# Keys scaled ahead of the scores, feed-forward sums tied to later tiles, attended sums by pairs, and a split exponential in a decoder layer

## The chip, the cores and the metric

The kernel runs on one core of a Trainium2 chip. The metric is the device time of one launch in microseconds (us); lower is better. The times of the kernel before are 1092.79, 1094.14 and 1094.13 us, median 1094.13. The profile is of one more execution.

The core has a matrix engine (TensorE, rows PE for matmuls and PEld for the loads of their stationary operand), VectorE (DVE), ScalarE (ACT), GpSimd (POOL) and SyncE (SP), which here only issues DMAs. Each engine works through its own queue in order; semaphores order the engines against each other. Matmuls write to PSUM banks, which TensorE, VectorE and ScalarE reach.

## The reference, cut to what matters

One decoder layer, post-norm, for 2 batches of 512 tokens of width 512, all in float32:

```python
# self attention: 16 heads of 128, weights = codes * block scales
q, k, v = x @ wq + bq, x @ wk + bk, x @ wv + bv
attn = softmax(q @ k.T / sqrt(128))            # per head, 512 x 512
x = layernorm(x + (attn @ v) @ wo + bo)
# cross attention over 1024 memory rows, one head of 512
scores = coef * (x @ Wq.T) @ mem.T
scores = scores - max(scores)
thr = top_k(scores, 54)[..., -1:]              # the 54th largest of each row
att = softmax(where(scores < thr, -inf, scores))
x = layernorm(x + (att @ mem) @ Wo.T)
# feed-forward, 2048 wide
gate, up = split(x @ w_gate_up.T)
x = layernorm(x + (silu(gate) * up) @ w_down.T)
```

## The kernel before, in words

**Products with seven blocks.** Almost every matrix product goes through `seven` (L170 to 229). It cuts both operands in 2 x 2 blocks and makes the product of the blocks with seven block products instead of eight. Four extra sums of blocks are needed for the left operand (`combine_a`, L107 to 110) and four for the right one (`combine_b`, L116 to 119); they run on GpSimd or VectorE ahead of the product. The seven products go into four half banks: product 1 starts the bank `r`, products 6 and 7 add to it; products 2, 5 and 4 go into three parts of a double bank `z`, and product 3 adds to one of them. After each of the products 1, 6 and 7 ScalarE copies `r` to SBUF with a bias (`keep` 0, 1 and 2, L197; the tiles are named u, for instance uqk). Product 3 of one call is left open (`open_product`) and is done by `close` inside the next call, after its product 6, so that it need not wait. VectorE then adds z and u: `on_second` makes one half of the result, `on_first` the other. In the profile the rows of L187 are these products: rqk, zqk for queries and keys, rv and zv for values, ro and zo for the output product, rxq and zxq for the query of the cross attention, rgu and zgu for the feed-forward's gate and up, rpd and zpd for its down product.

**Self attention.** 32 units: 4 groups of 4 heads by 2 batches are 8 phases of 4 units. For each unit:
- `queries_keys` (L736): one call of `seven` makes the key k (add at L747, from keep 2) and the query q (add at L748). The first unit has its own function with plain matmuls.
- `weights` (L770): four score matmuls sc (L784), two tiles of 128 x 512 to a double bank; VectorE takes the negated row maximum of both (L795), ScalarE multiplies it by `HSCALE` (L796, the 1/sqrt(128) of the reference), and makes the exponential with the same scale and that bias (L799, with a sum per row), VectorE the reciprocal (L807), ScalarE the normalised weights (L808). VectorE turns blocks of 32 x 32 (L811) and 16 DMAs finish the transpose (tq to pt, L819).
- `attend` (L825): the attended values av (L831) of an earlier unit; ScalarE copies them to ot (L849). `project` (L860) does the sums otc of four units' ot (L116 to 119) and the output product of a phase, added to the residual (L876, L878).

The double bank z of the products and the double banks of scores come from the same two buffers. A product that takes a buffer waits until the exponentials of the score tiles in it are done.

**Cross attention.** `seven_xquery` makes the query of a batch, from x1T (the turned residual) and x1c (its four sums, on VectorE); `qc` are the sums of the query (L142, L143), the right operand of the scores. `clip` (L483) finds the 54th largest score of each row by seven rounds of MAX8 (L487, L496) and six of MATCH_REPLACE8 (L493) on a 128 x 1024 tile; ScalarE makes the exponential (L500), VectorE keeps those over the threshold and sums them (L502), and ScalarE scales by the reciprocal (L506). Batch 0's search runs beside the self attention of batch 1, that of batch 1 (`search1`) beside the feed-forward of batch 0. `xattend` does the rest of it.

**Feed-forward.** For each batch two halves of 8 units. `up` (L1077) loads weights wgu (L1104), makes the sums wc on GpSimd (L107 to 110), calls `seven`, adds the up half ut (L1121) and the gate half gt (L1127), takes the Silu (L1129), multiplies (L1130) and makes the sums hc for the next product. `load_wdn` brings the down weights, `combine_wdn` (L1056) makes their sums dc on GpSimd (L1067 to 1074, eight of 128 x 512), and `down` (L1146) the product. The calls stand at L1198 to 1230; `next(between)` in `up` gives the sums of `combine_wdn` out a piece at a time.

**What sets the order.** The program is written with the functions above, but each engine's order is not the order of the text: a planner takes all instructions with their dependences and orders them by estimated times. An added dependence or a longer instruction in one place can therefore move others. Buffers are named by tags (`place`, `bank`, `double`), and a tag's next tile waits for the last reader of the one before.

ScalarE has its functions in tables: where Exp, Silu or Sqrt follow one another, an ACT_TABLE_LOAD stands between (rows of L500 and L1129 among them). Identity and Copy need none.

Of the kernel before, what the change touches and what calls it, by code (L numbers as in the profile page):

```python
# [24 lines left out]
def decoder_layer(  # L25
# [52 lines left out]
    def place(tag, shape, name):  # L78
        return sb.tile([P, *shape], F32, tag=tag, name=name)
# [87 lines left out]
        if open_product:  # L167
            open_product.pop()()

    def seven(name, stat, mov, cols, on_second, on_first, bias=(0.0, 0.0), late=False, piece=None):  # L170


        n = seven_count[0] % 2
        seven_count[0] += 1
        r = bank("r", f"r{name}")[:, :HS]
        if piece:

            zs = [bank("t", f"z{name}_{i}")[:, :HS] for i in range(2)] + [double(f"z{name}", (4, HS))[:, 2, :]]
        else:
            z = double(f"z{name}", (4, HS))  # L180
            zs = [z[:, i, :] for i in range(3)]
        u = place(f"u{n}", (3, HS), f"u{name}")

        def product(i, o, start=True):
            left, right = chunks(stat[i]), chunks(mov[i])
            for k in range(len(left)):
                nc.tensor.matmul(  # L187
                    o,
                    left[k][:, cols],
                    right[k],  # L190
                    start=start and k == 0,
                    stop=k == len(left) - 1,
                    skip_group_check=not start,
                )

        def keep(i, at):
            nc.scalar.activation(u[:, i, :], r, AF.Identity, bias=at)  # L197

        if late:
            product(2, zs[1])  # L200
            product(4, zs[0])
        product(1, r)
        keep(0, bias[0])
        if not late:
            product(2, zs[1])
        product(5, zs[2])
        product(6, r, False)
        keep(1, bias[0])
        close()
        product(7, r, False)  # L210
        keep(2, bias[1])
        if piece:
            piece(zs[2], u[:, 2, :], 1, 1)
            piece(zs[1], u[:, 0, :], 0, 0)
        if not late:
            product(4, zs[0])
        if piece:
            piece(zs[0], u[:, 2, :], 1, 0)
        else:
            on_second(z[:, 0::2, :], u[:, 2:3, :].to_broadcast([P, 2, HS]))  # L220

        def rest():
            product(3, zs[2], False)
            if piece:
                piece(zs[2], u[:, 1, :], 0, 1)
            else:
                on_first(z[:, 1:3, :], u[:, 0:2, :])

        open_product.append(rest)
# [252 lines left out]

    def clip(b, t, tag):  # L483

        s = sts[b, t]
        top = small.tile([P, 8], F32, tag="top", name=f"top{b}_{t}")
        nc.vector.max(top, s)  # L487
        mx = small.tile([P, 1], F32, tag="mx", name=f"mx{b}_{t}")
        nc.vector.tensor_scalar_mul(mx, top[:, 0:1], -1.0)
        work = place(tag, (M,), f"work{b}_{t}")  # L490
        src = s
        for r in range((CLIP_K - 1) // 8):
            nc.vector.match_replace(work, top, src, LOWEST)  # L493
            src = work
            top = small.tile([P, 8], F32, tag="top", name=f"top{b}_{t}_{r}")
            nc.vector.max(top, work)  # L496
            yield
        at = (CLIP_K - 1) % 8
        e = work
        nc.scalar.activation(e, s, AF.Exp, bias=mx)  # L500
        sm = small.tile([P, 1], F32, tag="xsm", name=f"xsm{b}_{t}")
        nc.vector.scalar_tensor_tensor(  # L502
            s, s, top[:, at : at + 1], e, ALU.is_ge, ALU.mult, accum_out=sm
        )
        nc.vector.reciprocal(sm, sm)
        nc.scalar.activation(s, s, AF.Copy, scale=sm)  # L506
        yield

    def clips(b, tags):
# [226 lines left out]
    def queries_keys(u):  # L736

        g, b, j = units[u]
        h = g * GH + j
        qt = place(f"q{u % 2}", (2, HS), f"q{u}")  # L740
        kt = place(f"k{u % 2}", (2, HS), f"k{u}")
        seven(
            f"qk{u}",
            qkw[u],
            xcs[b],
            slice(0, P),
            lambda z, c: nc.vector.tensor_add(kt, z, c),  # L747
            lambda z, c: nc.vector.tensor_add(qt, z, c),  # L748
            (bq_sb[:, h : h + 1], bk_sb[:, h : h + 1]),
        )  # L750
        qs[u], ks[u] = qt.rearrange("p n s -> p (n s)"), kt.rearrange("p n s -> p (n s)")

    def first_queries_keys():

        z = double("zqk0", (2, S))
        for k in range(KD):
            for n in range(2):
                nc.tensor.matmul(
                    z[:, n, :],
                    raw["qk0"][0][:, k, n, :],  # L760
                    xts[0][:, k, :],
                    start=k == 0,
                    stop=k == KD - 1,
                )
        qs[0] = place("q0", (S,), "q0")
        ks[0] = place("k0", (S,), "k0")
        nc.scalar.activation(qs[0], z[:, 0, :], AF.Identity, bias=bq_sb[:, 0:1])
        nc.scalar.activation(ks[0], z[:, 1, :], AF.Identity, bias=bk_sb[:, 0:1])

    def weights(u):  # L770

# [2 lines left out]
        for t in range(NT):  # L774
            if t % 2 == 0:

                if u == 0 and t:
                    pair = [bank("t", f"sc{u}_{t}_{n}") for n in range(2)]
                else:
                    scs = double(f"sc{u}_{t}")  # L780
                    pair = [scs[:, n, :] for n in range(2)]
                nms = small.tile([P, 2], F32, tag="nm", name=f"nm{u}_{t}")
                for n in range(2):
                    nc.tensor.matmul(  # L784
                        pair[n],
                        q[:, (t + n) * P : (t + n + 1) * P],
                        k,
                        start=True,
                        stop=True,
                    )  # L790
                if u == 0 and t:
                    for n in range(2):
                        nc.vector.reduce_max(nms[:, n : n + 1], pair[n], axis=AX.X, negate=True)
                else:
                    nc.vector.reduce_max(nms, scs, axis=AX.X, negate=True)  # L795
                nc.scalar.mul(nms, nms, HSCALE)  # L796
            pr = place(f"p{t}", (S,), f"p{u}_{t}")
            sm = small.tile([P, 1], F32, tag="sm", name=f"sm{u}_{t}")
            nc.scalar.activation(  # L799
# [1 line left out]
                pair[t % 2],  # L801
                AF.Exp,
                bias=nms[:, t % 2 : t % 2 + 1],
                scale=HSCALE,
                accum_out=sm,
            )
            nc.vector.reciprocal(sm, sm)  # L807
# [17 lines left out]
    def attend(u):  # L825
# [14 lines left out]
        if j % 2 == 0:  # L840
# [11 lines left out]
            AF.Identity,  # L852
            bias=bv_sb[:, h : h + 1],
        )

    def combine_o(eng, p):
        w = raw[f"o{p}"][0]
        ow[p] = combine_a(eng, blocks_t(w), place("wv" if p == last else "cmb1", (4, GH // 2, HD), f"oc{p}"))

    def project(p):  # L860

        g, b = phases[p]
        lo, hi = ots.pop((p, 0)), ots.pop((p, 1))
        oc = combine_b(
            nc.vector,
            (lo[:, :, :HS], lo[:, :, HS:], hi[:, :, :HS], hi[:, :, HS:]),
            place("cmb0", (4, GH // 2, HS), f"otc{p}"),
        )
        rr = rb[b].rearrange("p (h s) (c f) -> p h s c f", h=2, c=2)
        for s in range(NT // 2):  # L870

# [24 lines left out]
    for k in range(KD):  # L896
        nc.scalar.dma_start(out=first[0][k], in_=wqk_first[0][:, k])
        nc.sync.dma_start(out=xts[0][:, k, :], in_=xT[0, k * P : (k + 1) * P, :])
    nc.sync.dma_start(out=bqkv_sb, in_=bqkv)
    for n in range(2):  # L900
        nc.scalar.dma_start(out=first[1][n], in_=wqk_first[1][:, n * HK : (n + 1) * HK])
    for h in range(2):
# [140 lines left out]

    NH = NI // 2
    NQ = NH // 2
    wdns = {}

    def load_wdn(b, half):
        wdns[b, half] = []
# [3 lines left out]
            nc.sync.dma_start(out=t, in_=rows.rearrange("(i p) f -> p i f", p=P))  # L1053
            wdns[b, half].append(t)

    def combine_wdn(b, half):  # L1056

        b00, b01, b10, b11 = (f[:, :, h] for f in wdns[b, half] for h in (slice(0, HD), slice(HD, D)))
        c = []
# [3 lines left out]
            c += [two[:, 0], two[:, 1]]  # L1063
        wdns[b, half] = BRIGHT((b00, b01, b10, b11), c)
        steps = [slice(k, k + 2) for k in range(0, NQ, 2)]
        for w in steps:
            nc.gpsimd.tensor_tensor(c[0][:, w], b01[:, w], b00[:, w], ALU.subtract)  # L1067
            yield
# [8 lines left out]
    def up(b, half, eng, search=iter(()), between=iter(()), other=None):  # L1077
# [23 lines left out]
        for n in range(NH):  # L1101
# [10 lines left out]
            if other and n == NH - 1:  # L1112
                for _ in search:
                    pass
                for _ in other:
                    if sums:
                        sums.pop()()
            ut = place(f"k{n % 2}", (2, HS), f"ut{i}_{b}")

            def second(z, u, ut=ut):  # L1120
                nc.vector.tensor_add(ut, z, u)  # L1121
# [80 lines left out]
    seven_xquery(1, "xT1", "xc1", ("sc1", "p0"))  # L1202
    score_tiles(1, (("v0", 2), ("v1", 2)))
    seven_xscores(1)
    for _ in chain(combine_wdn(0, 0), combine_mem(1, ("wqk2", "sc2", "p2", "p3"))):
        pass
    search1 = clips(1, ("work",))
    hc = up(0, 0, nc.gpsimd, search1)
# [3 lines left out]
    def attended_early():  # L1212
        xw["woc"] = combine_b(nc.gpsimd, blocks(xw["wo"]), place("v1", (4, HK, HD), "woc"))
        yield from xattend(1, ("ot0", "ot1"))

    hc = up(0, 1, nc.vector, search1, combine_wdn(0, 1), attended_early())
    layernorm(1, "b")
    turn_x(1, "v0", "v1", "x2T")
    combine_turned(nc.vector, 1, "v0", "x2")
# [1 line left out]
    close()  # L1221
    finish(0)
    load_wdn(1, 0)
    hc = up(1, 0, nc.vector, between=combine_wdn(1, 0))
    down(1, 0, hc)
    load_wdn(1, 1)
    hc = up(1, 1, nc.vector, between=combine_wdn(1, 1))
    down(1, 1, hc, True)
    close()
    finish(1)  # L1230
# [68 lines left out]
```

## Time and profile before

| | |
|---|---|
| runs, us | 1092.79, 1094.13, 1094.14 |
| the profiled execution, us | 1093.0 |
| its span, us | 1090.8 |
| granted TensorE clock | 1.0 |
| VectorE, row maxima L795 | 63 of 1223 ns |
| ScalarE, scaling of maxima L796 | 64 of 202 ns |
| ScalarE, exponentials of the attention L799 | 128 of 685 ns |
| GpSimd, weight sums of the feed-forward L107 | 32 of 774 ns |
| VectorE, searches of the cross attention L496, L493 | 48 of 1221 ns, 40 of 1208 ns |
| ScalarE, exponential of the search L500 | 8 of 1152 ns |

The span is the time from the first to the last instruction that the profiler saw; the execution's time contains a little around it. A row of the views gives start and duration, engine, line, operation, the tile written and the tiles read, with partitions x elements. What stands in brackets is the idle time of the engine before it and what ended that. Some 36 of the 4290 matmul records are missing from this trace, so sums over matmuls are a little low.

By time the span has these parts: up to 540 us self attention with batch 0's cross attention in between; 540 to 735 the last units of the self attention and batch 1's cross query; 735 to 910 the feed-forward of batch 0 with batch 1's search; then the end of its cross attention and the feed-forward of batch 1.

### The profile page before, as it was taken

What the parts mean: (1) busy time and instruction counts of PE and PEld (TensorE: products, weight loads), DVE (VectorE), ACT (ScalarE), POOL (GpSimd) and SP (SyncE); (2) the same over time, 40 slices, a digit from 0 to 9 for tenths busy, and PEclk for the clock granted to TensorE, in tenths of its full rate; (3) what the DMA queues carried; (4) which work ended last, traced back from release to release, by engine and by line L of the source; (5) the groups of instructions that cost most, each with busy time, mean ns of one, the idle gap of its engine ahead of it and who ended that gap; (6) DMA issues with size and microseconds to landing.
All of it is one profiled execution on the core that took longest, in us unless ns stands there. A gap on an engine that the chain in (4) does not pass through costs nothing.

```text
span 1090.8 us, 12892 instructions
## 1 busy us (share of the span) xinstructions
PE 1074.4 (98%) x4254; PEld 798.2 (73%) x4254; DVE 636.6 (58%) x1043; ACT 416.6 (38%) x945; POOL 546.2 (50%) x546
## 2 busy tenths in 40 slices
PE   9999999999999999999999999989999999999997
PEld 6676776677677677665666567668888888888886
DVE  5445445346345445643899874568999736543354
ACT  3454435335344443733444453321443214221221
POOL 4965715845843844513852553651675812454620
PEclk9999999999999999999999999999999999999999
DMA  9634536554554355535332535431214401422201
GB/s 350 193 101 154 193 103 210 183 160 154 179 172 127 124 185 155 185 90 179 135 116 78 154 102 208 133 97 42 80 65 145 134 22 50 164 78 77 96 20 39
DMA packets 66256, 142.70 MB, mean 131 GB/s; under 512 B 12560, under 2 KB 12560, under 8 KB 66192
## 3 DMA queue, kind: packets, MB, share of 16 engines
q1 hardware_dynamic: 65328, 139.80, 40.2%
q10 hardware_dynamic: 864, 2.10, 0.5%
q8 instruction: 34, 0.56, 0.2%
q14 instruction: 30, 0.25, 0.1%
HBM read 99.90 MB, written 2.10 MB: 94 GB/s over the span
## 4 chain that ended last, share of the span: by engine, by line
PE 77%; DVE 14%; ACT 4%; DMA 2%; issue 1%; POOL 1%; ACTq 0%; DVEq 0%; POOLq 0%; SPq 0%
PE sc L784 9%; PE av L831 9%; PE zqk L187 8%; PE zgu L187 7%; PE rqk L187 6%; PE rgu L187 5%; PE zo L187 5%; PE zv L187 5%; PE ro L187 4%; DVE work L493 4%; DVE top L496 3%; PE zpd L187 3%; PE rv L187 3%; PE rpd L187 3%; PE zxav L187 2%; PE rxav L187 2%
## 5 line engine op out<-in xcount | busy, mean ns | idle before, releaser
L831 PE MATMUL av<-pt,v 128*128 128x512 f32 x256 | 121.8, 592 | 0.0
L784 PE MATMUL sc<-k,q 128*128 128x512 f32 x256 | 116.9, 597 | 0.0
L795 DVE TENSOR_REDUCE nm<-sc 128x2 f32<-128x1024 f32 x63 | 76.8, 1223 | 66.9 <-PE sc L784 66.9
L811 DVE STREAM_TRANSPOSE tq<-p 128x512 f32<-128x512 f32 x128 | 85.0, 698 | 35.1 <-ACT p L808 27.9
L107 POOL TENSOR_TENSOR wc<-wqk 128x256 f32<-128x256 f32 x31 | 24.2, 782 | 161.9 <-PE zqk L187 160.9
L784 PEld LDWEIGHTS sc<-k,q 128*128 128x128 f32 x256 | 47.6, 190 | 58.0 <-issue 50.9
L684 POOL TENSOR_TENSOR wqk<-wqk,sqk 128x512 f32<-128x512 f32 x52 | 65.1, 1273 | 47.7 <-DMA wqk<-in_wqk 28.2
L799 ACT ACTIVATE p<-sc,nm 128x512 f32<-128x512 f32 x128 | 86.9, 685 | 1.5
L808 ACT ACTIVATE p<-p,sm 128x512 f32<-128x512 f32 x128 | 86.1, 722 | 0.6 <-DVE sm L807 0.6
L107 POOL TENSOR_TENSOR wc<-wgu 128x256 f32<-128x256 f32 x32 | 24.8, 774 | 102.4 <-PE zgu L187 41.5
L197 ACT ACTIVATE ugu<-rgu 128x256 f32<-128x256 f32 x96 | 36.2, 379 | 103.7 <-PE rgu L187 101.5
L831 PEld LDWEIGHTS av<-pt,v 128*128 128x128 f32 x256 | 48.6, 190 | 30.5 <-issue 26.8
L197 ACT ACTIVATE uqk<-rqk,bqkv_sb 128x256 f32<-128x256 f32 x93 | 44.0, 473 | 64.9 <-PE rqk L187 64.8
L187 PE MATMUL rgu<-x2c,wc 128*128 128x256 f32 x256 | 66.1, 380 | 1.0 <-ACT ugu L197 1.0
L187 PE MATMUL rqk<-x0c,wc 128*128 128x256 f32 x248 | 64.8, 384 | 0.3
L187 PEld LDWEIGHTS rqk<-x0c,wc 128*128 128x128 f32 x248 | 45.5, 190 | 19.4 <-ACT uqk L197 10.0
L496 DVE MAX8 top<-work 128x8 f32<-128x1024 f32 x48 | 58.6, 1221 | 0.9
L187 PEld LDWEIGHTS rgu<-x2c,wc 128*128 128x128 f32 x256 | 48.3, 190 | 8.7 <-ACT ugu L197 1.6
L849 ACT ACTIVATE ot<-av,bqkv_sb 128x512 f32<-128x512 f32 x28 | 19.2, 687 | 81.0 <-PE av L831 81.0
L493 DVE MATCH_REPLACE8 work<-top,work 128x1024 f32<-128x1024 f32 x40 | 48.3, 1208 | 0.0
L1127 DVE TENSOR_TENSOR gt<-zgu,ugu 128x512 f32<-128x512 f32 x32 | 21.9, 684 | 44.7 <-PE zgu L187 44.7
L684 POOL TENSOR_TENSOR wv<-wv,sv 128x512 f32<-128x512 f32 x24 | 29.9, 1272 | 29.7 <-DMA pt<-tq 26.7
(310 smaller groups left out, 2444.5 us busy)
## 6 DMA issues: line engine op xcount, KB each, us to landing
pt<-tq SPq DMA_DIRECT2D x512, 64.0 KB, 2.0
wgu<-in_wgu SPq DMA_DIRECT2D x32, 512.0 KB, 3.2
wqk<-in_wqk SPq DMA_DIRECT2D x26, 512.0 KB, 4.1
sqk<-in_wqk_s SPq DMA_DIRECT2D x26, 512.0 KB, 4.2
wdn<-in_wdn SPq DMA_DIRECT2D x8, 1024.0 KB, 5.7
sv<-in_wv_s SPq DMA_DIRECT2D x14, 512.0 KB, 5.8
wv<-in_wv SPq DMA_DIRECT2D x7, 1024.0 KB, 5.5
wo<-in_wo SPq DMA_DIRECT2D x7, 1024.0 KB, 5.6
```

The costliest lines, as they stand in the source:

```text
L107: eng.tensor_tensor(c[0], a10, a11, ALU.add)
L187: nc.tensor.matmul(o, left[k][:, cols], right[k], start=start and k == 0, stop=k == len(left) - 1, skip_group_check=not start,)
L197: nc.scalar.activation(u[:, i, :], r, AF.Identity, bias=at)
L493: nc.vector.match_replace(work, top, src, LOWEST)
L496: nc.vector.max(top, work)
L684: eng.tensor_tensor(part[:, w], codes[:, w], sct[:, w], ALU.mult)
L784: nc.tensor.matmul(pair[n], q[:, (t + n) * P : (t + n + 1) * P], k, start=True, stop=True,)
L795: nc.vector.reduce_max(nms, scs, axis=AX.X, negate=True)
L799: nc.scalar.activation(pr, pair[t % 2], AF.Exp, bias=nms[:, t % 2 : t % 2 + 1], scale=HSCALE, accum_out=sm,)
L808: nc.scalar.activation(pr, pr, AF.Copy, scale=sm)
L811: nc.vector.transpose(tq[:, :, :, t, :].rearrange("p n k c -> p k n c"), pr.rearrange("p (k n a) -> p k n a", n=NB, a=BLK),)
L831: nc.tensor.matmul(av, vs[u // GH][:, k, j * P : (j + 1) * P], pt[:, :, k, :], start=(k == 0), stop=(k == NT - 1),)
```

## The change

Four edits.

1. The key is scaled by `HSCALE` where it is made: its bias by a constant tile `bks`, the copy keep 2 by the activation's scale, and the addition of z by a scalar_tensor_tensor in place of an addition. The scaling of the row maxima (L796) and the scale of the exponential go.
2. `combine_wdn` gets a function `behind`. Before its sums, two small copies by GpSimd write a piece of a tile into the destination, so that the sums come after that tile: in the first group after a query sum of batch 1 (`qts[1][6]`, written at L143), in the other three after the newest up half ut.
3. The sums of the attended values are made in two halves of 256 columns, the first in `attend` once the phase's third unit is there, the second in `project`.
4. In `clip` the exponential and the last scaling are each made in two halves of 512 columns.

```diff
-    def seven(name, stat, mov, cols, on_second, on_first, bias=(0.0, 0.0), late=False, piece=None):
+    def seven(name, stat, mov, cols, on_second, on_first, bias=(0.0, 0.0), late=False, piece=None, scale=1.0):
...
-        def keep(i, at):
-            nc.scalar.activation(u[:, i, :], r, AF.Identity, bias=at)
+        def keep(i, at, scale=1.0):
+            nc.scalar.activation(u[:, i, :], r, AF.Identity, bias=at, scale=scale)
...
-        keep(2, bias[1])
+        keep(2, bias[1], scale)
...
         e = work
-        nc.scalar.activation(e, s, AF.Exp, bias=mx)
+        halves = [slice(n * half_m, (n + 1) * half_m) for n in range(2)]
+        for w in halves:
+            nc.scalar.activation(e[:, w], s[:, w], AF.Exp, bias=mx)
...
-        nc.scalar.activation(s, s, AF.Copy, scale=sm)
+        for w in halves:
+            nc.scalar.activation(s[:, w], s[:, w], AF.Copy, scale=sm)
...
-            lambda z, c: nc.vector.tensor_add(kt, z, c),
+            lambda z, c: nc.vector.scalar_tensor_tensor(kt, z, HSCALE, c, ALU.mult, ALU.add),
             lambda z, c: nc.vector.tensor_add(qt, z, c),
-            (bq_sb[:, h : h + 1], bk_sb[:, h : h + 1]),
+            (bq_sb[:, h : h + 1], bks[:, h : h + 1]),
+            scale=HSCALE,
...
-        nc.scalar.activation(ks[0], z[:, 1, :], AF.Identity, bias=bk_sb[:, 0:1])
+        nc.scalar.activation(ks[0], z[:, 1, :], AF.Identity, bias=bks[:, 0:1], scale=HSCALE)
...
-                nc.scalar.mul(nms, nms, HSCALE)
...
-                scale=HSCALE,
...
+        if j == GH // 2:
+            combine_ot(u // GH, 0)
...
+    def combine_ot(p, k):
+
+        lo, hi = ots[p, 0], ots[p, 1]
+        if k == 0:
+            otcs[p] = place("cmb0", (4, GH // 2, HS), f"otc{p}")
+        combine_b(
+            nc.vector,
+            [f[:, k, h] for f in (lo, hi) for h in (slice(0, HS), slice(HS, S))],
+            otcs[p][:, :, k],
+        )
...
+        combine_ot(p, 1)
         lo, hi = ots.pop((p, 0)), ots.pop((p, 1))
-        oc = combine_b(
-            nc.vector,
-            (lo[:, :, :HS], lo[:, :, HS:], hi[:, :, :HS], hi[:, :, HS:]),
-            place("cmb0", (4, GH // 2, HS), f"otc{p}"),
-        )
+        oc = BRIGHT((lo[:, :, :HS], lo[:, :, HS:], hi[:, :, :HS], hi[:, :, HS:]), [otcs[p][:, n] for n in range(4)])
...
+    bks = const.tile([P, H], F32, name="bks")
+    nc.scalar.mul(bks, bk_sb, HSCALE)
...
-    def combine_wdn(b, half):
+    def combine_wdn(b, half, behind):
...
+        for n in (0, 2):
+            nc.gpsimd.tensor_copy(c[n][:, ::2, 0:1], behind())
...
             ut = place(f"k{n % 2}", (2, HS), f"ut{i}_{b}")
+            uts[:] = [ut]
...
-    for _ in chain(combine_wdn(0, 0), combine_mem(1, ("wqk2", "sc2", "p2", "p3"))):
+    for _ in chain(combine_wdn(0, 0, lambda: qts[1][6][:, :, 0:1]), combine_mem(1, ("wqk2", "sc2", "p2", "p3"))):
...
-    hc = up(0, 1, nc.vector, search1, combine_wdn(0, 1), attended_early())
+    hc = up(0, 1, nc.vector, search1, combine_wdn(0, 1, lambda: uts[0][:, :, 0:1]), attended_early())
...
-    hc = up(1, 0, nc.vector, between=combine_wdn(1, 0))
+    hc = up(1, 0, nc.vector, between=combine_wdn(1, 0, lambda: uts[0][:, :, 0:1]))
...
-    hc = up(1, 1, nc.vector, between=combine_wdn(1, 1))
+    hc = up(1, 1, nc.vector, between=combine_wdn(1, 1, lambda: uts[0][:, :, 0:1]))
```

The order in which each engine's instructions stand in the changed kernel is known before it runs, since the planner sets it. TensorE has as many instructions as before (2145), VectorE 1021 for 989, ScalarE 784 for 825 with 21 table loads for 15, GpSimd 559 for 551, and SyncE 773 as before.

More of the change, by code (lines that the diff above doesn't have):

```diff
@@ L858, in combine_o @@
         ow[p] = combine_a(eng, blocks_t(w), place("wv" if p == last else "cmb1", (4, GH // 2, HD), f"oc{p}"))
+    otcs = {}
+    def combine_ot(p, k):
[7 more added lines that the diff above has]
+        )
     def project(p):
         g, b = phases[p]
+        combine_ot(p, 1)
         lo, hi = ots.pop((p, 0)), ots.pop((p, 1))
-        oc = combine_b(
-            nc.vector,
-            (lo[:, :, :HS], lo[:, :, HS:], hi[:, :, :HS], hi[:, :, HS:]),
-            place("cmb0", (4, GH // 2, HS), f"otc{p}"),
-        )
+        oc = BRIGHT((lo[:, :, :HS], lo[:, :, HS:], hi[:, :, :HS], hi[:, :, HS:]), [otcs[p][:, n] for n in range(4)])
         rr = rb[b].rearrange("p (h s) (c f) -> p h s c f", h=2, c=2)
@@ L1045, in decoder_layer @@
     NQ = NH // 2
-    wdns = {}
+    wdns, uts = {}, []
     def load_wdn(b, half):
```

## Prediction

> All steps are in microseconds and are summed against the profiled execution, 1093.0 (its span is 1090.8; the rest lies around it). That is 1.1 below the median of the runs shown, 1094.13, and I add the 1.1 at the end. A difference under 0.2%, 2.2, can't be told from no change.
>
> **What bounds it.** First the page, its busy shares and its chain:
>
> ```profile
> PE 1074.4 (98%) x4254; PEld 798.2 (73%) x4254; DVE 636.6 (58%) x1043; ACT 416.6 (38%) x945; POOL 546.2 (50%) x546
> ...
> PE 77%; DVE 14%; ACT 4%; DMA 2%; issue 1%; POOL 1%; ACTq 0%; DVEq 0%; POOLq 0%; SPq 0%
> ```
>
> TensorE is never long idle, so the end moves only where a matmul waits. The change removes no matmul. I took from the timeline the distances between matmul starts: 216 ns for 256 columns, 430 for 512. The recorded matmuls at that pace make 1055; what is above pace are stalls: 12.4 between 8 and 540 (attention), 14.1 from there to 1085. Only these can be won. Next, the view of waits, for TensorE's weight loads (total, times, longest):
>
> ```profile
> PEld rqk L187 <- ACT uqk L197: 10.0, 13, 0.9
> ...
> PEld sc L784 <- DVE q L748: 5.1, 16, 0.4
> PEld zqk L187 <- ACT p L799: 4.9, 12, 0.4
> ...
> PEld zv L187 <- ACT p L799: 3.2, 7, 0.6
> ```
>
> These totals contain the ordinary pace; above pace they are 2.90, 2.38, 1.83 and 2.29. The third and fourth are the ones that the change touches: the products' double bank is still read by the exponential of the unit's first two score tiles.
>
> **Keys scaled.** One place of that kind, in the timeline (start, duration):
>
> ```profile
> 183.54 0.20 ACT L796 ACTIVATE nm<-nm 128x2 f32<-128x2 f32 x1 [3.15 <-DVE nm L795]
> ...
> 185.28 0.73 PEld L187 LDWEIGHTS zqk<-x0T,wqk 128*128 128x128 f32 x4 [0.42 <-ACT p L799]
> ```
>
> The row maximum is ready at 183.50, its scaling starts at 183.54, the first exponential at 183.78; the second one's accumulator is out at 185.23, and the product that by pace was due at 185.09 starts at 185.28. With the stall carried into the next product that is 0.29. Without the scaling the exponentials start 0.24 earlier: about 0.05 stays. Over the 14 groups that wait so (1.83 + 2.29 = 4.1) I take **-3.5**; bounds 0 and -4.1. Six more groups between 540 and 660 have 1.1 of such stall, three of them labelled with the key addition: **-0.5**.
>
> What is late next: in the instruction order of the changed kernel ScalarE does, per unit, two exponentials, keep 0, one exponential, three normalisations, the last exponential, keep 1 and the rest. Keep 1 ends, counted from the last score matmul's end by the rows' durations, at about 5.12; and product 7, which there no longer has an attended product ahead of it, wants it at 5.16. So a wait of 0.0 to 0.2 in many units takes the place of 0.29 in ten (2.90 now): **0**, bounds -1.5 and +3.
>
> The key addition becomes a scalar_tensor_tensor on 31 units. Plain it takes 0.68 (row of L747). The nearest row is L502's, 1.26 for 1024 columns when alone, 1.55 mean: 0.63 to 0.78 for 512. The key has about 0.2 of room before the scores. **0**; if that cover goes, 31 x 0.1 = 3. The constant's scaling is one small ScalarE instruction (0.2, as L260's on the same tile) that waits, as L260's does until 10.64, for the biases' DMA: 0.
>
> **Attended sums by pairs.** 8 sums of 256 columns for 4 of 512 in each phase: 8 x 0.42 (the 256-column sums of L1097) for 4 x 0.69, 0.6 more on VectorE, which is 58% busy, and half of it four units' worth earlier. No matmul row waits on these sums. **0**, bounds -0.9 (all stalls on L876, which is queued behind them) and +0.6.
>
> **Down sums behind, first group.** VectorE (start, duration), where the second query starts, and TensorE:
>
> ```profile
> 714.79 1.76 DVE L118 TENSOR_TENSOR x1c<-x1T 128x512 f32<-128x512 f32 x1
> 716.47 1.75 DVE L117 TENSOR_TENSOR x1c<-x1T,x1c 128x512 f32<-128x512 f32 x1
> ```
> ```profile
> 718.33 0.73 PEld L187 LDWEIGHTS rxq<-x1c,wqc 128*128 128x128 f32 x4 [2.17 <-POOL dc L1067]
> 719.95 0.73 PEld L187 LDWEIGHTS zxq<-x1c,wq 128*128 128x128 f32 x4 [0.89 <-DVE x1c L119]
> ```
>
> The label names GpSimd, but these matmuls read x1c. The same sum takes 0.68 at 714.19; while GpSimd's down sums run (714.38 to 725.9) it takes 1.75. Two of them late by 1.07 are the 2.03 above pace at 718.33, and 0.75 follows. After the change these sums wait for the query's sums, which stand behind the same matmuls: 2.03 + 0.75 = 2.78, less a little, **-2.6**; bounds -3.7 (0.95 at 729.86 too) and -1.5. The sums then run at about 732.7 to 744.5 (the GpSimd order puts one set of weight sums ahead of them), beside VectorE's four x2c sums of 739.8 to 742.9. Two of these at +1.07 would be 2.1, partly ahead of need: **+0.7**, bounds 0 and +2.1. The tiny copies are below the 0.73 of the shortest GpSimd sum and hide in its idle half. SyncE issues the same DMAs, a few in another order: 0.
>
> **Down sums behind, later groups.** A copy that waits for the second unit's up half stands ahead of eight sums and of the fifth unit's weight sums in GpSimd's queue. In the last group of batch 1 the up half is there at 1024.5; 8 x 1.27 and three weight sums end at 1037.4, wanted at 1038.0: covered by 0.6. In the first of batch 1 five sums stand ahead: covered by some 5. In the second group of batch 0 not:
>
> ```profile
> 849.80 1.46 POOL L1074 TENSOR_TENSOR dc<-wdn,dc 128x512 f32<-128x512 f32 x1
> 851.21 0.72 POOL L107 TENSOR_TENSOR wc<-wgu 128x256 f32<-128x256 f32 x1
> ```
>
> Now two of the sums are done at 823.9 and six take 1.27 to 2.25 (mean 1.57) around the fourth unit's weights. Afterwards all eight start with the up half of 842.1: at 1.57 they end at 854.7, the fifth unit's four weight sums at 857.6, three of the output weights' at 861.6, three more weight sums at 863.7; TensorE wants that at 860.6. That is +3.1; at 1.27 apiece it is +0.7. I take **+1.7**.
>
> **Search in halves.** The counts of the order show what the diff does not: table loads on ScalarE go from 15 to 21. All six fall into batch 0's feed-forward, in three of the four search tiles, where the order puts a Silu between the exponential's halves. The rows:
>
> ```profile
> 837.36 1.15 ACT L500 ACTIVATE work<-s,mx 128x1024 f32<-128x1024 f32 x1 [2.44 <-DVE top L496]
> 838.42 0.36 ACT L197 ACTIVATE ugu<-rgu 128x256 f32<-128x256 f32 x1
> 838.80 1.28 ACT L1129 ACT_TABLE_LOAD   x1
> 840.09 0.60 ACT L1129 ACTIVATE sg<-gt 128x512 f32<-128x512 f32 x1
> ```
>
> 838.80 + 1.28 = 840.08: the next activation follows at once, and the load starts 0.02 after the keep. Here a rule speaks against the change: the Trainium skill, "ScalarE: Activation LUTs", section "What ACT_TABLE_LOAD costs", counts 1.28 for the load and 1.38 for a drain, 2.66 for every switch, and its section on table sets asks for calls batched by set. By the rule six switches are 16.0 of ScalarE, by the trace 6 x 1.30 = 7.8. The load agrees, the drain is not seen; I use 1.30. ScalarE is idle there most of the time, so what counts is which keep falls behind a load. A unit takes 6.04, and its keeps start 2.53, 1.73 and 1.79 apart; each must be out before the next product into the shared bank, so they can be late by about 0.9, 0.1 and 2.0 before TensorE waits (estimates from the 0.38 of a keep and the 0.86 of a product). First tile: VectorE gets the exponential two loads later and the up half comes 1.2 late against 1.1: +0.1. Second: one keep up to 2 late, +1.5, less the 0.57 that waits there now. Last: the keep behind the whole exponential (0.96 now) gets free, and the transposes' sums end about 0.8 late: 0. Together **+1.0**, bounds -1.5 and +7.8.
>
> **Sum.** 1093.0 - 3.5 - 0.5 - 2.6 + 0.7 + 1.7 + 1.0 = 1089.8; with 1.1, **1090.9**.
>
> **Rivals.**
> Slower: the six table loads land whole. Place: ScalarE beside the search, where VectorE is busy 37 to 39 of each 40 and catches up nothing. For: keep 1 has 0.1 of slack, and VectorE's sums wait for both halves. Against: ScalarE is mostly idle, and waits of now go. All of 7.8 instead of 1.0 gives 1097.7; the rule's 16.0, 1105.9. It decides from about 1.1 per load that reach TensorE (1096.3 less 1089.9 without them, over six).
> No change: the attention's gain is taken back by keep 1 and product 7 (4.0 lost), all else as summed: 1094.9. For: 5.12 against 5.16. Against: keep 1 then starts earlier in absolute terms than now.
> Larger gain: keep 1 is in time and half of its 2.90 goes, and loads and GpSimd's block cost 0: 1090.9 - 1.5 - 2.7 = 1086.7.
> That the change doesn't do what it says is out: the order shows no scaling of maxima left, and the copies ahead of the sums.
>
> **Numbers.** Forecast 0.50, its own range 1088.5 to 1093.5, a fifth of it within 0.2%; larger gain 0.11; no change 0.19; slower 0.20. Faster is 0.40 + 0.11 = 0.51, same 0.10 + 0.19 = 0.29, slower 0.20. The range runs from 1085.5 to 1098.0; about 0.06 is left below, 0.10 above.
>
> **What would show it.** Right: no maxima scaled, waits of zqk and zv on the exponential under 1 above pace; the x1c sums all at 0.7 and no gap at 718; table loads 21; one gap of 1 to 3 at the fifth unit of batch 0's second half, released by GpSimd's weight sums. Wrong: a wait of rqk on the keep in every unit, over 0.2 each; or gaps in units beside the search that sum to over 6.

## The result and the profile after

The changed kernel takes 1110.78 us (median; 1108.14 to 1111.89), the kernel before 1094.14: 1.0154 times the time, interval 1.0130 to 1.0178. It is 16.6 us slower where 3.2 us less were forecast. The profiled execution has a span of 1109.7 us, 18.9 more than before. Its busy shares and the chain that ended last:

```profile
PE 1080.6 (97%) x4254; PEld 802.0 (72%) x4254; DVE 652.7 (59%) x1075; ACT 418.9 (38%) x904; POOL 544.8 (49%) x554
...
PE 75%; DVE 12%; ACT 6%; DMA 3%; issue 2%; POOL 1%; SPq 1%; DVEq 0%; ACTq 0%; POOLq 0%
```

TensorE does the same matmuls. VectorE is 16 us busier for 32 more instructions, which is far more than 32 small sums should take. That is the first thing to follow. I summed the distances between matmul starts above the ordinary pace, over the whole span: 28.7 us of stalls became 47.5. The 18.8 more are the whole loss of the profiled execution: 11.5 of them lie between 8 and 540 us (attention), 7.1 after that, the rest in the first 8 us. The waits of TensorE's weight loads (total, times, longest):

```profile
PEld sc L789 <- DVE q L752: 10.5, 16, 0.8
PEld zqk L187 <- POOL wqk L688: 5.9, 3, 2.7
...
PEld zqk L187 <- ACT p L803: 5.0, 7, 1.0
PEld rqk L187 <- ACT uqk L197: 4.9, 12, 0.6
...
PEld zqk L187 <- POOL wv L688: 2.7, 1, 2.7
PEld zgu L187 <- POOL wc L107: 2.6, 1, 2.6
...
PEld zv L187 <- ACT p L803: 1.7, 8, 0.3
```

The zv waits are down, as forecast (3.2 before). New are long waits of zqk, up to 2.7 us, and one of zgu. GpSimd's name on the zqk ones is misleading. Here is one in the timeline of VectorE, with the rows of GpSimd, ScalarE and the weight loads for the same place (start, duration, engine), and last the row maxima of the kernel before at that place:

```profile
166.24 0.79 DVE L117 TENSOR_TENSOR otc<-ot,otc 128x256 f32<-128x256 f32 x1 [1.75 <-ACT ot L852]
166.95 1.48 DVE L118 TENSOR_TENSOR otc<-ot,ot 128x256 f32<-128x256 f32 x1
168.36 1.48 DVE L119 TENSOR_TENSOR otc<-ot,otc 128x256 f32<-128x256 f32 x1
169.76 2.34 DVE L800 TENSOR_REDUCE nm<-sc 128x2 f32<-128x1024 f32 x2
```
```profile
166.71 5.48 POOL L688 TENSOR_TENSOR wv<-wv,sv 128x512 f32<-128x512 f32 x4
```
```profile
171.01 0.69 ACT L803 ACTIVATE p<-sc,nm 128x512 f32<-128x512 f32 x1 [4.81 <-DVE nm L800]
171.60 0.19 ACT L803 ACTIVATION_READ_ACCUMULATOR p<-sc,nm 128x1 f32 x1
171.69 0.68 ACT L803 ACTIVATE p<-sc,nm 128x512 f32<-128x512 f32 x1
172.26 0.20 ACT L803 ACTIVATION_READ_ACCUMULATOR p<-sc,nm 128x1 f32 x1
```
```profile
172.53 0.51 PEld L187 LDWEIGHTS zqk<-x0T,wqk 128*128 128x128 f32 x3 [2.72 <-POOL wv L688]
```
```profile
167.57 1.23 DVE L795 TENSOR_REDUCE nm<-sc 128x2 f32<-128x1024 f32 x1 [2.74 <-PE sc L784]
```

The rows show a chain. The pair sums of the attended values wait on VectorE for ot. Two of them take 1.48 us where 0.41 is usual; GpSimd makes its sums of wv at the same time, four in 5.48. The row maxima of the next scores stand behind the pair sums in VectorE's queue and start at 169.76; in the kernel before, the same maxima start 1.9 us after the first score matmul (167.57 after 165.66), which would be 167.2 here. The exponentials follow, and the product that needs their bank starts right after the second accumulator is out, at 172.46. GpSimd's sum, which the label names, ended at 172.19, but zqk does not need it. The same gap, 2.16 above pace, is at 253.81 and at 335.14.

The same trace holds a phase in which GpSimd is idle at that place:

```profile
409.23 0.42 DVE L118 TENSOR_TENSOR otc<-ot,ot 128x256 f32<-128x256 f32 x1
409.56 0.42 DVE L119 TENSOR_TENSOR otc<-ot,otc 128x256 f32<-128x256 f32 x1
409.90 1.22 DVE L800 TENSOR_REDUCE nm<-sc 128x2 f32<-128x1024 f32 x1
```
```profile
410.85 2.50 POOL L688 TENSOR_TENSOR wqk<-wqk,sqk 128x512 f32<-128x512 f32 x2 [22.18 <-DMA wqk<-in_wqk]
```

The sums stand ahead of the maxima here too, but they are quick, the maxima start 1.9 us after the first score matmul (407.97), and zqk follows without a gap. So the place in the queue alone does no harm; place and slow sums together do.

The second half of the sums stands ahead of the maxima as well, in five phases (106, 188, 269, 349 and 428 us), with gaps of 0.8 to 1.8, 5.1 together. These are not the pairs' doing: with scaled keys and whole sums ("Keys alone", below) the same five gaps are there, 5.0 together.

The sums by shape, before and after (count, busy, mean ns):

```profile
L119 DVE TENSOR_TENSOR otc<-ot,otc 128x512 f32<-128x512 f32 x7 | 7.4, 1062 | 0.0
```
```profile
L118 DVE TENSOR_TENSOR otc<-ot,ot 128x256 f32<-128x256 f32 x14 | 12.7, 910 | 0.0
L119 DVE TENSOR_TENSOR otc<-ot,otc 128x256 f32<-128x256 f32 x14 | 10.6, 757 | 0.0
L117 DVE TENSOR_TENSOR otc<-ot,otc 128x256 f32<-128x256 f32 x14 | 9.9, 706 | 18.3 <-ACT ot L852 18.3
L116 DVE TENSOR_TENSOR otc<-ot 128x256 f32<-128x256 f32 x14 | 5.6, 436 | 0.0
```

Half the columns, and three of the four sums take more than 0.69 us, the usual time of 512 columns. Counting all 64 half sums of the trace, the 33 with no GpSimd sum beside them took 0.41 to 0.43; the 31 beside one took 1.05 on average and up to 1.49. Already before, one of four had a mean of 1.06 where 0.69 is usual: it met GpSimd.

The second new wait, in batch 0's second half of the feed-forward, on GpSimd and on TensorE:

```profile
864.24 1.72 POOL L1090 TENSOR_TENSOR dc<-wdn,dc 128x512 f32<-128x512 f32 x1
865.91 1.72 POOL L1092 TENSOR_TENSOR dc<-wdn,wdn 128x512 f32<-128x512 f32 x1
867.59 1.71 POOL L1094 TENSOR_TENSOR dc<-wdn,dc 128x512 f32<-128x512 f32 x1
869.26 1.17 POOL L107 TENSOR_TENSOR wc<-wgu 128x256 f32<-128x256 f32 x1
```
```profile
867.15 1.13 PE L187 MATMUL zgu<-x2T,wgu 128*128 128x256 f32 x4 [0.83 <-DVE gt L1148]
870.48 2.07 PE L187 MATMUL zgu<-x2c,wc 128*128 128x256 f32 x4 [2.20 <-POOL wc L107]
872.35 1.91 PE L187 MATMUL rgu<-x2c,wc 128*128 128x256 f32 x4
874.06 1.91 PE L187 MATMUL zgu<-x2T,wc 128*128 128x256 f32 x4
```

The eight down sums run in a block until 869.3, the weight sums come after, and TensorE waits 2.4 us above pace. Then groups of four matmuls take 1.91 instead of 1.03. The table by stretch shows why (length; busy of PE, PEld, DVE, ACT, POOL; granted clock; DMA share; GB/s):

```profile
172.00:180.00 8.00, 7.44 (x24) 5.56 (x24) 3.92 (x10) 5.55 (x13) 2.69 (x3) 0.79 0.53 209
...
336.00:343.00 7.00, 6.84 (x28) 4.72 (x26) 3.88 (x8) 4.03 (x9) 3.88 (x5) 1.00 0.53 172
868.00:878.00 10.00, 7.80 (x23) 6.07 (x22) 5.94 (x9) 1.60 (x5) 9.84 (x11) 0.66 0.16 42
```

After the gaps at 172 and 870 the clock was granted at half for a while; after the gap at 335, as long as that at 172, it was not.

### The profile page after: what moved, and what is told of

Same layout as the page of the kernel before. It is cut to its first block, busy times and chain, and to the rows that moved or that the text cites. A ratio compares the mean times of both kernels' runs of the same rounds, so it can differ in the third digit from the quotient of the medians.

```text
span 1109.7 us, 12812 instructions
## 1 busy us (share of the span) xinstructions
PE 1080.6 (97%) x4254; PEld 802.0 (72%) x4254; DVE 652.7 (59%) x1075; ACT 418.9 (38%) x904; POOL 544.8 (49%) x554
## 4 chain that ended last, share of the span: by engine, by line
PE 75%; DVE 12%; ACT 6%; DMA 3%; issue 2%; POOL 1%; SPq 1%; DVEq 0%; ACTq 0%; POOLq 0%
PE zgu L187 8%; PE av L834 8%; PE zqk L187 8%; PE rgu L187 6%; PE sc L789 6%; PE rqk L187 5%; PE zo L187 5%; PE zpd L187 4%; PE zv L187 4%; PE rpd L187 3%; PE ro L187 3%; PE rv L187 3%; ACT p L803 2%; PE zxav L187 2%; DVE work L494 2%; DVE nm L800 2%
## 5 line engine op out<-in xcount | busy, mean ns | idle before, releaser
L752 DVE TENSOR_TENSOR q<-zqk,uqk 128x512 f32<-128x512 f32 x31 | 21.4, 689 | 39.4 <-PE zqk L187 39.2
```

## The experiments

Each was timed beside the kernel before on the same chip; "by" is the ratio to it, with its interval. The planner finds an order for each kernel anew, so an edit can move work elsewhere. First the four parts, each alone in the kernel before; their edits are the hunks of the diff above.

### Keys alone

> Only the keys are scaled in advance; the rest is as before. Theory (the loss of the changed kernel is VectorE's pair sums ahead of the row maxima): the scaled keys cost nothing and bring part of what was forecast, 1089 to 1093, with the zqk and zv waits on the exponential under 1.5 us above pace. Rival (the keys themselves are at fault, through keep 1 in every unit or the dearer key addition): 1096 or more, with a rqk wait on the keep over 0.2 in most units.

Measured: 1096.38 us for 1093.61, by 1.0028 (1.0017 to 1.0039). The rival's time, but not its trace: the scaled addition takes 688 ns for 681, and the waits of rqk on the keep are 2.45 above pace for 2.90. The zv waits went from 2.29 to 0.61, as forecast. Five waits of zqk, one in each of five phases, grew from about 0.29 to between 0.6 and 1.75, 5.0 together. Up to 540 us this makes 1.2 more of stalls than before. Another 2.2 came between 540 and 660 us (4.4 became 6.6); the largest gap there, 0.94 at 599 us, is a rqk that waits for a keep, so there the rival is right in part. One of the five, on VectorE and ScalarE:

```profile
178.98 0.69 DVE L117 TENSOR_TENSOR otc<-ot,otc 128x512 f32<-128x512 f32 x1 [0.89 <-ACT ot L848]
179.59 1.22 DVE L118 TENSOR_TENSOR otc<-ot,ot 128x512 f32<-128x512 f32 x1
180.73 1.21 DVE L796 TENSOR_REDUCE nm<-sc 128x2 f32<-128x1024 f32 x1
```
```profile
181.97 0.69 ACT L799 ACTIVATE p<-sc,nm 128x512 f32<-128x512 f32 x1 [3.02 <-DVE nm L796]
```

The sums are whole here, and again they stand ahead of the maxima. The order without the scaling instruction puts the last attended product right before the scores. In the kernel before, two products and half of a third stand between, and the sums are done by then.

### Pairs alone

> Only the attended sums are made by pairs. Theory: both halves of the sums wait for an attended tile on VectorE with the row maxima queued behind them, so that the exponentials and then the next product are late by 1 to 2 us in most phases: 1102 to 1110, and phases with a stall over 2 us are followed by a few us of matmuls at half pace. Rival (the sums are hidden, as forecast; the loss is the table loads or GpSimd's block): 1093 to 1095.

Measured: 1105.03 us, by 1.0108 (1.0093 to 1.0123), as the theory had it. Gaps of zqk of 1.30, 2.39, 2.38 and 1.73 above pace at 172, 252, 332 and 604 us, and eight matmuls at half pace after one of them.

### Down sums behind, alone

> Only the down sums are put behind. Theory: 2.6 us are won at the second cross query, 2 to 3 us are lost at the fifth unit of the second half of batch 0, where TensorE waits for the weight sums, and about 3 more after it if the matmuls go on at half pace: 1094 to 1098. Rival (GpSimd's block is the main loss): over 1102. Rival (the block is covered): 1091.

Measured: 1094.47 us, by 1.0007 (1.0001 to 1.0014). Stalls in the three places: 712 to 745 us, 4.06 before and 2.17 now; 840 to 870, 0.08 and 5.18; batch 1, 2.20 and 1.12. So 1.9 and 1.1 are won and 5.1 lost; the loss is the wait (2.1 at its first matmul), some seven matmuls at half pace after it, and a late up half before it.

### Search in halves, alone

> Only the exponential and the last scaling of the search are made in halves; six table loads more. Theory: the loads cost TensorE little, 1093 to 1097. Rival (the six loads are the main loss): 1101 or more, with gaps beside the search released by ScalarE or by VectorE's sums there.

Measured: 1095.11 us, by 1.0016 (1.0009 to 1.0022): in the theory's range. Most of the added stalls are at 643 us (1.4 for 0.3) and at 717 to 725 (the cross query's wait on x1c twice, then half pace), places that the loads do not touch. Beside the search, from 745 to 890 us, 2.4 became 3.0.

The four ratios add up to 1.0159, the changed kernel's is 1.0154.

### The changed kernel with whole sums

```diff
-        if j == GH // 2:
-            combine_ot(u // GH, 0)
...
-        combine_ot(p, 1)
...
+        oc = combine_b(
+            nc.vector,
+            (lo[:, :, :HS], lo[:, :, HS:], hi[:, :, :HS], hi[:, :, HS:]),
+            place("cmb0", (4, GH // 2, HS), f"otc{p}"),
+        )
```

> The changed kernel with the attended sums made whole again. Theory (the parts add up, and the pair sums are 11.4 of the 16.6 us): 1093.6 + 2.8 + 0.9 + 1.5 = 1098.8, so 1097 to 1101. Rival (the parts work on each other through the order that the planner finds for all of them): under 1096, or over 1103.

Measured: 1098.26 us, by 1.0050 (1.0038 to 1.0063). The parts add up (1.0028, 1.0007 and 1.0016 make 1.0051). The pairs are 1.04% of the changed kernel, 11.4 us (1.0154 less 1.0050, by the ratios, since before was 1.1 us faster in this round).

### Keys, with the sums behind the row maxima

The sums are called after the scores of the unit; a copy by VectorE of the maxima into their destination keeps them behind:

```diff
+                maxima[0] = nms
...
+        if maxima[0] is not None:
+            for n in (0, 2):
+                nc.vector.tensor_copy(c[:, n, 0, 0:2], maxima[0])
         combine_b(
...
             weights(u)
+            if p < last and j in (GH - 1,):
+                combine_ot(p, j - 2)
```

> Keys scaled, and the attended sums (whole) tied by a copy of two columns to the unit's last row maxima, so that on VectorE they come after them. Theory (in the run with scaled keys alone it is the attended sums ahead of the row maxima that delay the exponentials, 5.0 us of stalls against 1.8): 1089 to 1092.5. Rival (the scaled keys are slower by themselves, by the keeps): 1095 to 1098, as without the tie.

Measured: 1089.74 us for 1093.06, by 0.9967 (0.9956 to 0.9979), as the theory had it. The waits that the scaled keys were to remove are now gone (total, times, longest):

```profile
PEld zqk L187 <- ACT p L802: 1.9, 8, 0.4
PEld zv L187 <- ACT p L802: 1.5, 8, 0.2
```

Above pace they are 0.21 and 0.45, for 1.83 and 2.29 before: 3.46 won.

### Pairs, with the sums behind the row maxima

The same tie, in the kernel before, for each half after its unit.

> Attended sums by pairs alone, each half tied to the row maxima in the same way. Theory (their place ahead of the row maxima is the whole loss): 1093 to 1096. Rival (it is their number or the contention with GpSimd): 1101 or more, as without the tie.

Measured: 1101.35 us, by 1.0084 (1.0069 to 1.0099). The theory missed: place ahead of the maxima is not the whole loss. VectorE, GpSimd, ScalarE and TensorE at the largest gap, 3.9 us above pace:

```profile
95.92 1.45 DVE L116 TENSOR_TENSOR otc<-ot 128x256 f32<-128x256 f32 x1
97.29 0.15 DVE L810 RECIPROCAL sm<-sm 128x1 f32<-128x1 f32 x1
97.36 1.42 DVE L118 TENSOR_TENSOR otc<-ot,ot 128x256 f32<-128x256 f32 x1
98.70 1.48 DVE L117 TENSOR_TENSOR otc<-ot,otc 128x256 f32<-128x256 f32 x1
100.10 0.15 DVE L810 RECIPROCAL sm<-sm 128x1 f32<-128x1 f32 x1
```
```profile
97.04 2.86 POOL L684 TENSOR_TENSOR wqk<-wqk,sqk 128x512 f32<-128x512 f32 x2
```
```profile
100.28 0.72 ACT L811 ACTIVATE p<-p,sm 128x512 f32<-128x512 f32 x1 [2.09 <-DVE sm L810]
100.91 0.46 ACT L197 ACTIVATE uqk<-rqk,bqkv_sb 128x256 f32<-128x256 f32 x1
```
```profile
101.42 2.07 PE L187 MATMUL rqk<-x0c,wc 128*128 128x256 f32 x4 [3.75 <-ACT uqk L197]
```

Now the reciprocals are behind the sums, the normalisation waits for them, keep 1 stands behind the normalisation, and product 7 waits for keep 1. In a phase where GpSimd is idle (179 us) the same four sums take 0.41 to 0.43 each and the gap there is 0.31, as before. So it takes two things: a sum at 1.45 us beside GpSimd, and something urgent behind it.

### Pairs on GpSimd

```diff
         combine_b(
-            nc.vector,
+            nc.gpsimd,
```

> Attended sums by pairs alone, but made by GpSimd, not by VectorE. Theory, as it stands after the tied pairs were still 8 us slower (a sum on VectorE takes 1.45 in place of 0.42 us while GpSimd has a sum of its own, and whatever waits behind it on VectorE, the maxima or the reciprocals, is late by that): without them on VectorE the attention is as before, 1091 to 1096. Rival (the pairs cost because the output product's operand or TensorE's order is another one): 1099 or more.

Measured: 1091.76 us for 1093.63, by 0.9983 (0.9977 to 0.9990): as the theory had it, and a little faster than before; where that little is won its trace does not show, for its profiled execution took 1092.9. On GpSimd the sums take their plain time:

```profile
L118 POOL TENSOR_TENSOR otc<-ot,ot 128x256 f32<-128x256 f32 x14 | 10.2, 727 | 0.0
```

The attention's stalls are 12.55 us, before 12.42; the output product's operand and the number of sums cost nothing as long as the sums are not on VectorE.

### Down sums behind in three groups

```diff
-    hc = up(0, 1, nc.vector, search1, combine_wdn(0, 1, lambda: uts[0][:, :, 0:1]), attended_early())
+    hc = up(0, 1, nc.vector, search1, combine_wdn(0, 1), attended_early())
```

> The down sums put behind in three groups, all but the second half of batch 0. Theory (that group costs about 5 us, its stall and the matmuls at half pace after it, while the first group wins 2 to 3): 1089 to 1091.5. Rival (the gain of the first group is taken back by the later sums, wherever the second group is): 1093 to 1095.

Measured: 1090.56 us for 1093.06, by 0.9979 (0.9970 to 0.9988). Against all four groups (1.0007) the one left out is 0.28%, 3.1 us.

### The search of batch 1 alone in halves

```diff
-        halves = [slice(n * half_m, (n + 1) * half_m) for n in range(2)]
+        halves = [slice(n * half_m, (n + 1) * half_m) for n in range(2)] if b else [slice(0, M)]
```

> Search in halves for batch 1 alone, that is the six table loads without the change in batch 0's search, which runs beside the attention and needs none. Theory (in the run with all halves the stalls that were added lie at 643 and at 717 us, from batch 0's search and a changed order, and the loads themselves give back what they take): within 1 us of before, 1092 to 1094. Rival (the loads are the cost): 1094.5 to 1096, with the gaps beside the search.

Measured: 1093.19 us for 1093.63, by 0.9996 (0.9987 to 1.0004), with all 21 table loads. But not quite for the reason given: the stalls from 745 to 890 us went from 2.4 to 3.3, so the loads and what they shift cost 0.9; the gap at 718 us, 2.03 before, is gone because here three of the four x1c sums are all but done (713.75 to 715.63) when GpSimd's down sums start (715.29, after 714.38 before). The loads in the changed kernel's ScalarE row:

```profile
778.11 1.28 ACT L503 ACT_TABLE_LOAD   x1
779.40 0.72 ACT L503 ACTIVATE work<-s,mx 128x512 f32<-128x512 f32 x1
780.14 1.28 ACT L1150 ACT_TABLE_LOAD   x1
```

A load of 1.28 and the next activation 0.01 after it; the load after the exponential starts 0.02 after that one's end.

### Versions that beat both

Scaled keys with whole sums tied, and the down sums behind in three groups:

> Scaled keys, whole attended sums tied behind the row maxima, down sums behind in three groups. If the parts add up: 1093.1 - 3.3 - 2.5 = 1087.3, so 1086 to 1089. If the two gains overlap (one wait replaces the other): 1089 to 1091.

Measured: 1088.28 us for 1093.63, by 0.9948 (0.9936 to 0.9961).

Scaled keys, pairs on GpSimd, and the down sums behind in three groups:

> Scaled keys, attended sums by pairs on GpSimd, down sums behind in three groups; the search whole. If the gains add up (the untied keys lost only through the attended sums on VectorE, which are gone from there): 1093.6 - 3.5 - 1.9 - 2.5, so 1084 to 1088. If GpSimd is late with its other sums, or the scaled keys lose in another way: 1089 to 1095.

Measured: 1088.00 us for 1093.37, by 0.9958 (0.9944 to 0.9971), at the edge of the first range; no better than the tied sums. One output product at 421 us now waits 1.33 for a sum on GpSimd.

## Why the prediction was wrong, by its steps

**Attended sums by pairs: 0, bounds -0.9 and +0.6.** This is the step that failed. It measured 11.4 alone (1105.03 less 1093.61), and as much within the change. It said "No matmul row waits on these sums", which asks who reads the result. The question that decides is who stands behind the instruction in its queue: the row maxima, and through them the exponentials, the bank and the next product. And it priced a sum at 0.42 from a row where GpSimd was idle. Four hints were in the profile before: GpSimd is 50% busy, the x1c sums took 1.75 beside it (the prediction used this one itself, two paragraphs further), one of four sums of this very tile had a mean of 1.06, and three of the four wait for the newest ot. The Trainium skill has a rule for the slow sums in "SBUF — State Buffer", section "Who interferes with whom": a VectorE instruction with two SBUF inputs contends with a GpSimd instruction that reads SBUF, and one with at most one SBUF input, outside the faster modes, does not. The sums read SBUF twice. The trace agrees: 1.48 for 0.41, while the maxima, which read PSUM, took 1.22 with and 1.21 without GpSimd beside them. The delay follows GpSimd's instruction, not VectorE's: a half sum takes 1.48 beside a GpSimd sum of 128x512 and 0.94 beside one of 128x256, and beside 128x512 the delay is 1.07 for 256 columns (1.48 less 0.41) as for 512 (1.75 less 0.68, the x1c sums). So a sum cut in half can pay it twice.

**Keys: -3.5 and -0.5, and 0 for what is late next.** The first term was right to 0.04 once nothing stood in front (3.46 measured with the sums tied). The second did not come: between 540 and 660 us the stalls of 4.4 became 6.6 with the keys alone and 5.0 with the sums tied. Up to 540 us the keep did not become the bound (2.1 to 2.8 above pace for 2.90), and the dearer addition was 7 ns. But alone the keys cost 2.8 us where 4.0 were to be won. The prediction saw in the order that the attended product now stands right before the scores, and drew from it only that product 7 comes sooner. The other end of that move, ot and so the sums later and ahead of the maxima, was left out.

**Down sums, first group: -2.6 + 0.7.** Right: 4.06 became 2.17, which is -1.9. The last term came as 1.22 at 742 us. Another 1.1 was won in batch 1, at 938 us, which was not counted.

**Down sums, second group: +1.7, from 0.7 to 3.1.** The wait was right in place and cause, and near in size (2.1 alone, 2.7 in the changed kernel, with its second matmul). Not priced was the half clock after it, 2.0 to 2.9 us more; stalls of the stretch grew by 5.1, and leaving the group out gave back 3.1 in time.

**Search in halves: +1.0.** Right in size for the loads: 0.6 to 0.9 beside the search. The drain that the Trainium skill, "ScalarE: Activation LUTs", section "What ACT_TABLE_LOAD costs", counts with each load isn't seen in this trace, and the rival that built on the loads, 1097.7 or more, is out: with all six of them the time is 0.9996 of before. The rest of the 1.5 us that all halves cost lies in batch 0's search, where the prediction costed nothing, and in a changed order around 717 us.

**The sum.** By parts, forecast and measured alone: pairs 0 and +11.4, keys -4.0 and +2.8, down sums -0.2 and +0.9, search in halves +1.0 and +1.5; together -3.2 and +16.6.

**The rivals.** Slower had 0.20, with the wrong mechanism. No rival asked what VectorE does between ot and the maxima.

Open: why the order changes where it does was not traced, only that it did; what slows the scaled keys between 540 and 660 us was not tried; and no gap was timed again to see how much of the clock's half grant is chance.

## What to carry to other kernels

For every instruction that is added or moved, list what stands behind it on its engine, not only who reads its result; work that is never on the path by its data can hold up the path by its place. Price a VectorE sum of two SBUF operands twice, alone and beside a GpSimd sum, and take the one that its place in the timeline says. Then measure the parts of a bundled change alone: here two of four parts win once other costs are out of their way, a third does on another engine, and the whole lost 16.6 us.

## What was not expected of the hardware

TensorE's clock can fall to half after a short gap. Counting all traces of this study, 11 gaps of TensorE had 1.86 to 3.75 us without a matmul; after 7 of them 7 to 13 matmuls ran at about half pace (427 instead of 216 ns), which cost 1.5 to 2.9 us more. Four had no such tail, among them one of 2.53 us. The changed kernel has three gaps of 1.92, two with the tail and one without, and once 1.81 was enough, soon after another gap. The Trainium skill, "TensorE: Matmul & The Clock Gate", section "What's actually happening", has the clock at half after an idle window of about 3.4 us that runs free of the program; that it depends on more than the gap's length agrees with the traces, but gaps well under 3.4 us were enough here, and the measurement decides.

In the run with the tied pairs, two copies of two columns by VectorE took 0.80 us together beside GpSimd (at 95 us), and 0.20 where GpSimd was idle (at 179 us).
